# Router logits of thirteen batches as row products on VectorE, and another order of the expert lists with four of the given tiles behind a branch

## The chip, the cores and the metric

The kernel runs on one core of a Trainium2 chip. The metric is the device time of the whole program in microseconds (us), the median of several runs. Instructions run on five engines, each with its own queue: TensorE (PE; its weight loads are shown apart as PEld), VectorE (DVE), ScalarE (ACT), GpSimd (POOL) and SyncE (SP), which here only issues transfers. An engine works its queue in order: what stands behind a waiting instruction waits too.

## The reference

The input x has 16 batches of 256 tokens with 256 features (D); ctx has the same shape. The layers follow each other, each added to x:

```
x = x + xattn0(ctx, layernorm(x))   # 8 heads of 128; keys and values from ctx and x: 512 rows
x = x + ffn0(layernorm(x))          # 1024 hidden units; weights plus a rank-one part made from 16 tokens of the batch
x = x + xattn1(layernorm(x), ctx, ctx)   # one head over 256 rows of ctx
x = x + experts(layernorm(x))       # 8 experts, weights by a router
```

The change touches the last layer. Its router and its experts are:

```
inh = sigmoid(y @ Wr / temperature)       # y = layernorm(x), Wr is 256 x 8: eight logits a token
dist = |inh - 1/e|;  in_zone = lower <= inh <= 0.5
w = exp(-dist/0.1) * in_zone              # zero for experts outside of the zone
w = (two nearest experts with exp(-dist/0.3), where no expert is in the zone);  w = w / sum(w)
out = sum over e of w[e] * (silu(y @ Wg[e]) * (y @ Wu[e])) @ Wd[e]
```

A token needs only the experts with w above zero. The matrices of an expert are 256 x 256. All data are 32-bit floats.

## The kernel before

**Batches and heads.** 16 batches of 8 heads make 128 steps. A step n issues, in this order, the scores of head n (`s1`, PE product `sc`), the division of its softmax rows by their sums on POOL (`s1_scale`), the fetch of the turned rows of head n-1 (`s2_fetch`, `pT`), the queries and keys of head n+1 (`s0q`, `s0k`, `pq` and `pk`), the products with the values of head n-2 (`s3`, `po`), and the turning of head n's rows (`s2`). Turning takes three pieces: DVE transposes blocks of 32 x 32 (`tb`), one transfer of SyncE writes them to DRAM (`hop`), and four transfers read them back in the other order (`pT`). The values `pv` and the preparation of later batches (`inputs`) are spread over the steps by `bulk`. A step takes some 11.3 us, a batch some 91 us.

**What runs between.** The program is written out in a fixed order (no scheduler moves anything). Between the pieces of a step, `gap` (L114) fills in pieces of a list of jobs: each job is a generator that yields the time after which its next piece may be issued, by a rough clock that counts the PE work issued so far (`Clock.pe`, advanced in `mm`, L79, through which every product goes: so nearly all products have line L80; the transposes on PE have L84). For each batch there are two jobs, added when the next batch is at its head 2 (`add_chain`, L1177): `chain(b)` (L345), the rest of that batch's layers, and `route(b)` (L712), its routing.

**The chain of a batch.** In order: the projection `px`; a layer norm; the rank-one part of the feed-forward weights, for which eight rows are written to DRAM and read back as a broadcast to all 128 rows of SBUF (`ev`, two halves of 512 KB; a fetch that is put in `behind_fetch` is issued right behind a head's `pT` fetch) and from which DVE makes `W1e` and POOL and DVE make `W2e`; the products `ph` and `pf`; the second attention (`pq1`, `sc1`, `po1`), for which DVE also makes one product of each row of y with a vector, summed along the row (L551); then the store of x, the layer norm whose rows stand in the tile `row` (256 features, 8 weights, 1 token number), the logits `pl` (L630) and their scaling by 1/temperature into `z` (L637). For the logits of batches 0 to 13 the rows are turned as above (`to_blocks` to `hop_yd_b`, `from_blocks` into `raw`, two copies to `ydT` by `evict`, which takes ACT or DVE by the rough clock); batches 14 and 15 are turned on PE (`turned_tile`, L365). Eight products of 128 x 8 follow with `Wr_sb`. The chain of batch b waits at three places for the chain of batch b-1: before the layer norm of the feed-forward part until `ph` of b-1 is issued (`A.fed`), before od/W1e until `pf` of b-1 is (`A.fed_forward`), and at L522 until the whole chain of b-1 is done. Tiles share buffers by tag: `W1e` has one buffer, and `q1T` is shared by q1T and ydT.

**The routing of a batch.** `route(b)` turns z into the weights (some 30 small operations on ACT and DVE), counts the tokens of each expert with the product `pn`, and gives each token a slot in a list of each expert in DRAM (`slots_d`): 16 indirect transfers on POOL (L804), each of 128 rows of 1060 bytes. A token that an expert doesn't serve is written to the end of that expert's list.

**The experts.** Batches 0 to 11 make part 0, 12 to 15 part 1. The first 1280 rows of each expert's list in part 0 (10 tiles of 128), and the first 512 in part 1 (4 tiles), are always worked; tokens beyond these limits fill spare "given" tiles, six in part 0 and one in part 1 (`UNITS`), whose expert and place are only known at run time (`plan`, L646; class `U`, suffix `_u`). What the given tiles cannot hold goes to loops behind `If beyond` at the end (class `V`). `experts` (L1444) walks a list of groups of one to four tiles (class `G`): a group's rows are loaded (`rows`, three groups ahead), turned through DRAM (`send_rows` two groups ahead: DVE transposes, then `hop_rows_b` on SyncE; `fetch_rows`: `yTd`), and then come the gate `pg` and up `pu` products, `hTd` on DVE, the down products `pd`, one or two groups later, and one indirect transfer per tile on POOL that adds 128 rows to out (L1317). A given tile is turned by PE (`yT_u`, two transposes), has its products `pg_u`, turns h (`hT_u`), and ends with `pd_u` and an indirect transfer; `experts` puts the pieces of a given tile between those of the groups next to it. The order of the lists is:

```
first = groups(0, (4, 3, 3), range(E - 1)) + groups(0, (3, 2, 2, 1, 1, 1), [E - 1])
second = len(first) - 4
lists = first[:-4] + groups(1, (4,), range(E - 1)) + first[-4:-3]
lists += groups(1, (2, 2), [E - 1]) + first[-3:]
units = {second - 1: U(1, 0)}
```

so the last groups of before are a pair of expert 7's part 0, two pairs of its part 1 and three single tiles, and the six given tiles of part 0 stand beside the first six groups of part 1. The last chain and the last routing are also issued into this list, as jobs beside it.

## Time and profile before

| | us |
|---|---|
| median of 3 runs | 1813.56 (1812.45 to 1814.58) |
| profiled execution, own time | 1817.54 |
| its span, first to last instruction | 1815.8 |
| PE busy | 1788.6 (98%) |
| DVE busy | 1201.5 (66%) |
| POOL busy | 838.0 (46%) |
| ACT busy | 589.2 (32%) |
| first and last logits product (`pl`) | 258.8 and 1574.5 |
| routing's transfers (L804), x256 | 291.2 to 1666.5, 962 ns each |
| given tiles' gate and up products (`pg_u`), x28 | 1681.2 to 1768.6, 592 ns each |
| PE clock, mean | 0.998 |

The profile is of one execution, by the hardware's own records. Its page gives for each engine the time in which it ran something ("busy"), the span in 40 slices, the chain of work that ended last, and groups of instructions by line and operation. A line such as "L80 PE MATMUL po<-pT,v 128*128 128x256 f32 x1024 | 242.6, 380 | 3.6" reads: products issued at line 80 that write tile po from tiles pT and v, 1024 of them, busy 242.6 us in sum, 380 ns each in the mean; the engine sat idle 3.6 us in sum just before them, and what follows names the operation that ended that idle time. Products are pipelined: their busy times overlap, so what one costs in a row of them is the distance from its start to the next start. The timeline shows one row for each run of like instructions: start in us, duration, engine and operation, and in square brackets the wait before it.

### The profile page before, as it was taken

Reading aid. Unit: us, or ns where it says so; the run is one execution under the profiler, and the core shown is the slowest. Engines: PE = TensorE matmul, PEld = TensorE weight load, DVE = VectorE, ACT = ScalarE, POOL = GpSimd, SP = SyncE. Lnnn points to the kernel's source line nnn. Section 1 sums busy time; section 2 is a strip of 40 time slices with the busy share of each in tenths; the row PEclk is TensorE's granted clock in tenths of the full one; section 3 lists DMA queues with packets and bytes.
Section 4 is the critical chain, followed back from the end, with each engine's and each line's share of the span. In section 5 each row is a group of like instructions: output and inputs, shape, how many; then the busy total and the mean of one; then the engine's idle time right before and its main releaser. Section 6 shows DMA issues by size and latency. Waiting matters only on the chain.

```text
span 1815.8 us, 22647 instructions
## 1 busy us (share of the span) xinstructions
PE 1788.6 (98%) x6540; PEld 1213.2 (67%) x6540; DVE 1201.5 (66%) x3346; ACT 589.2 (32%) x1316; POOL 838.0 (46%) x983
## 2 busy tenths in 40 slices
PE   8999999999999999999999999999999999999997
PEld 4566676767666666666666666666666677666566
DVE  5465576767676767676767676767666667675554
ACT  3442424243434343434343333333333311211111
POOL 2122225353535344534453435353534357676675
PEclk9999999999999999999999999999999999999999
DMA  6653546565656555656565555556545668899986
GB/s 221 183 180 117 179 133 200 156 197 159 194 162 195 161 190 166 198 158 189 167 191 165 182 173 178 173 181 175 179 153 170 185 179 225 201 252 229 232 158 97
DMA packets 265160, 326.07 MB, mean 180 GB/s; under 512 B 31900, under 2 KB 217672, under 8 KB 265032
## 3 DMA queue, kind: packets, MB, share of 16 engines
q1 hardware_dynamic: 235560, 274.21, 50.3%
q0 software_dynamic: 29424, 50.36, 11.8%
q8 instruction: 54, 0.88, 0.2%
q14 instruction: 74, 0.61, 0.1%
q10 hardware_dynamic: 48, 0.01, 0.0%
HBM read 162.45 MB, written 162.00 MB: 179 GB/s over the span
## 4 chain that ended last, share of the span: by engine, by line
PE 94%; DMA 3%; POOL 1%; DVE 1%; SPq 1%; issue 1%; ACT 0%; POOLq 0%; DVEq 0%; ACTq 0%
PE po L80 14%; PE sc L80 13%; PE pv L80 13%; PE pk L80 12%; PE pq L80 7%; PE px L80 6%; PE ph L80 6%; PE pf L80 6%; PE pg L80 5%; PE pd L80 5%; PE pu L80 5%; DMA hop<-tb 1%; PE pl L80 1%; PE pg_u L80 1%; DMA yTd<-hop_rows_b 1%
## 5 line engine op out<-in xcount | busy, mean ns | idle before, releaser
L980 ACT ACTIVATE pr<-sc,nm 128x512 f32<-128x512 f32 x256 | 173.5, 682 | 483.3 <-DVE nm L974 483.0
L988 POOL TENSOR_SCALAR pr<-pr,ri 128x512 f32<-128x512 f32 x256 | 179.0, 709 | 326.8 <-DVE ri L987 322.3
L804 POOL DMA_INDIRECT slots_d<-row,at_slot x256 | 254.6, 995 | 70.4 <-issue 69.5
L80 PE MATMUL po<-pT,v 128*128 128x256 f32 x1024 | 242.6, 380 | 3.6 <-DVE W2T L1041 1.5
L80 PE MATMUL sc<-kT,qT 128*128 128x512 f32 x512 | 241.0, 593 | 1.5 <-ACT kT L913 1.5
L80 PEld LDWEIGHTS po<-pT,v 128*128 128x128 f32 x1024 | 193.6, 190 | 72.7 <-issue 38.1
L80 PE MATMUL pk<-kvT,Wk_sb 128*128 128x512 f32 x512 | 240.6, 592 | 0.0
L80 PE MATMUL pv<-Wv_sb,kvT 128*128 128x512 f32 x512 | 235.0, 592 | 0.0
L1026 DVE TENSOR_SCALAR outT<-po,cvec 128x256 f32<-128x256 f32 x128 | 61.0, 477 | 242.1 <-PE po L80 242.0
L996 DVE STREAM_TRANSPOSE tb<-pr 128x512 f32<-128x512 f32 x256 | 165.8, 685 | 17.2 <-DMA hop<-tb 17.0
L80 PEld LDWEIGHTS pv<-Wv_sb,kvT 128*128 128x128 f32 x512 | 97.1, 190 | 108.2 <-issue 103.0
L974 DVE TENSOR_REDUCE nm<-sc 128x1 f32<-128x512 f32 x256 | 160.2, 662 | 2.0 <-PE sc L80 1.9
L80 PEld LDWEIGHTS sc<-kT,qT 128*128 128x128 f32 x512 | 97.0, 190 | 69.8 <-issue 61.2
L80 PEld LDWEIGHTS pk<-kvT,Wk_sb 128*128 128x128 f32 x512 | 97.3, 190 | 67.8 <-issue 61.2
L80 PE MATMUL pq<-kvT,Wq_sb 128*128 128x256 f32 x512 | 133.2, 383 | 0.0
L80 PEld LDWEIGHTS pq<-kvT,Wq_sb 128*128 128x128 f32 x512 | 96.6, 191 | 41.8 <-issue 28.2
L80 PE MATMUL px<-Wo_sb,outT 128*128 128x256 f32 x512 | 121.8, 381 | 0.0
L80 PE MATMUL ph<-ybT,W1e 128*128 128x256 f32 x512 | 121.0, 379 | 0.0
L1317 POOL DMA_INDIRECT out_dram<-o,at x65 | 101.8, 1567 | 37.7 <-DVE o L1316 9.3
L450 POOL TENSOR_TENSOR W2e<-ev,od 128x256 f32<-128x256 f32 x120 | 78.5, 681 | 87.7 <-DMA ev<-ev_d 87.7
L80 PE MATMUL pf<-W2e,hT 128*128 128x256 f32 x512 | 118.0, 379 | 0.0
L911 ACT COPY v<-pv 128x512 f32<-128x512 f32 (+1 forms) x132 | 70.6, 536 | 145.4 <-PE pv L80 145.4
(256 smaller groups left out, 2726.6 us busy)
## 6 DMA issues: line engine op xcount, KB each, us to landing
hop<-tb SPq DMA_DIRECT2D x128, 512.0 KB
pT<-hop SPq DMA_DIRECT2D x512, 128.0 KB
ev<-ev_d SPq DMA_DIRECT2D x32, 512.0 KB
rows<-slots_d SPq DMA_DIRECT2D x14, 530.0 KB
hop_rows_b<-rows_b SPq DMA_DIRECT2D x13, 512.0 KB
yTd<-hop_rows_b SPq DMA_DIRECT2D x52, 128.0 KB
rows<-slots_d SPq DMA_DIRECT2D x15, 397.5 KB
hop_rows_b<-rows_b SPq DMA_DIRECT2D x14, 384.0 KB
```

The costliest lines, as they stand in the source:

```text
L80: nc.tensor.matmul(out, lhsT, rhs, **kw)
L450: (nc.gpsimd if b < B - 1 else nc.vector).tensor_tensor(W2e[:, c, d, :].rearrange("p (i a) -> p i a", i=NI), evs[1][:, :, c * NA : (c + 1) ...
L804: ins = nc.gpsimd.indirect_dma_start(out=slots_d[part], out_offset=bass.IndirectOffsetOnAxis(ap=at_slot[:, c, e : e + 1], axis=0), in_=row ...
L911: nc.scalar.copy(out, src)
L974: nc.vector.tensor_reduce(nm, sc, AX.X, ALU.max, negate=True)
L980: nc.scalar.activation(pr, sc, AF.Exp, bias=nm, accum_out=sm)
L988: nc.gpsimd.tensor_scalar(pr, pr, ri, 1.0, ALU.mult, ALU.mult)
L996: nc.vector.transpose(tb[:, :, c, :], heads[n][c][0].rearrange("p (m f) -> p m f", m=QP))
L1026: nc.vector.tensor_scalar(o, po, col("bv", h), None, ALU.add)
L1317: ins = nc.gpsimd.indirect_dma_start(out=out_rows[0 : sum(NTOKS[: self.part + 1]), :], out_offset=bass.IndirectOffsetOnAxis(ap=self.at[:, ...
```

## The change

Four things change.

**Logits.** Batches 0 to 12 (`b < B - 3`) no longer turn the rows of the last layer norm and make no `pl`. The router matrix is copied once, at batch 0's head 5, into a DRAM tile `WrT_d` with a row for each expert (L1167). For each of these batches SyncE broadcasts it to all 128 rows of SBUF in two halves of 512 KB (`Wr_all`, in the buffer of `W1e`, fetched behind a head's pT), and DVE makes 16 row products with sums (L653: for each expert and half batch, 256 elements a row), whose sums are the logits. They are then scaled by 1/temperature. The elementwise products go to an unused tile in the buffer of `q1T`. Batch 13 now takes the way of 14 and 15: turned on PE, then `pl`.

**Waits.** The chain of b-1 need not be done at L531 (L522 before), only its second attention (`A.attended`); two new waits hold the making of `W1e` until the logits of b-2 are issued, and of `q1T` until those of b-1 are (`A.scored`). `Wr_all` is made only once `ph` of the next batch is issued (`A.fed`), since they share a buffer.

**Given tiles.** Two of part 0's six given tiles and the one of part 1 stay in the list (`AMONG`). The other four are worked at the end behind a branch, which is taken if the tokens beyond the limits need more than two tiles in part 0 or one in part 1; the loops of class `V` stand in a second branch inside it. `plan` makes a second flag, and both are loaded into registers.

**Lists.** Expert 7's part 0 is cut into 3, 2, 1, 1, 1, 1, 1. The five single tiles stand one by one behind the groups of four of part 1, from expert 2 to expert 6; the two pairs of part 1 of expert 7 end the list. The two given tiles of part 0 stand beside the first two groups of part 1.

```diff
--- before.py
+++ after.py
@@ -163,6 +163,8 @@
     NTOKS = [n * S for n in PARTS]
     CAPS = [10 * P, 4 * P]
     UNITS = (6, 1)
+    AMONG = (2, 1)
     NU = sum(UNITS)
     NM = max(n - k for n, k in zip(NTOKS, CAPS)) // P
@@ -248,6 +250,10 @@
     g0 = keep.tile([P, 1], F32, name="g0")
     WvT = keep.tile([P, DC, D], F32, name="WvT")
     Wr_sb = keep.tile([P, DC, E], F32, name="Wr_sb")
+    WrT_d = dram.tile([E, D], F32, tag="WrT_d", bufs=1, name="WrT_d")
+    zero = keep.tile([P, 1], F32, name="zero")
+    nc.gpsimd.memset(zero, 0.0)
@@ -427,6 +433,9 @@
             yield 0.2
         yield max(landed[0], there) - Clock.pe
         while behind is not None and b - 1 not in A.fed_forward:
+            yield 0.4
+        while b >= 2 and b - 2 not in A.scored:
             yield 0.4
@@ -519,7 +528,7 @@
         rs = ln_rstd(mv, "q")
         yield queued - 0.3
-        while behind is not None and not behind.done:
+        while behind is not None and b - 1 not in A.attended:
             yield 0.4
         y = wk.tile([P, TC, D], F32, tag="y", name=f"yc_{b}")
         ln_apply(y, x_b, mv, rs)
@@ -553,6 +562,8 @@
                 scale=1.0, scalar=g0, accum_out=rc[:, c : c + 1],
             )
         yield there - Clock.pe
+        while behind is not None and b - 1 not in A.scored:
+            yield 0.4
         q1T = wk.tile([P, DC, S], F32, tag="q1T", name=f"q1T_{b}")
         for m in range(DC):
             pq = mm_tile(S, f"pq1_{b}_{m}")
@@ -601,6 +612,7 @@
                 x_b[:, c, :], po, ri, x_b[:, c, :], ALU.mult, ALU.add
             )
             stats(c, "d", mv)
+        A.attended.add(b)
         rs = ln_rstd(mv, "d")
@@ -611,33 +623,58 @@
         row = A.row[b] = wk.tile([P, TC, ROW], F32, tag="row", bufs=2, name=f"row_{b}")
         ln_apply(row[:, :, 0:D], x_b, mv, rs)
         nc.vector.tensor_copy(row[:, :, D + E], number[:, b * TC : (b + 1) * TC])
-        if hopped:
-            hop = to_blocks(wk, row, TC, "tbc", 2, f"yd_{b}_b")
-            yield SENT
-            raw = raw_tile("raw_c", f"ydT_{b}")
-            from_blocks(raw, hop)
-            yield LANDED
-            ydT = wk.tile([P, DC, S], F32, tag="q1T", name=f"ydT_{b}")
-            for d in range(DC):
-                evict(ydT[:, d, :], in_order(raw)[:, d], None, None)
-            yield 4.0
+        if b < B - 3:
+            while b + 1 not in A.fed:
+                yield 0.4
+            Wr_all = wk.tile([P, E, D], F32, tag="W1e", name=f"Wr_all_{b}")
+            landed = []
+            def wr_everywhere(half):
+                nc.sync.dma_start(
+                    Wr_all[:, ts(half, E // 2), :].rearrange("p e d -> p (e d)"),
+                    WrT_d[ts(half, E // 2)].rearrange("e d -> (e d)").partition_broadcast(P),
+                )
+                landed.append(Clock.pe + 8.0)
+            behind_fetch.extend([lambda: wr_everywhere(0), lambda: wr_everywhere(1)])
+            while b >= 1 and b - 1 not in A.weighed:
+                yield 0.4
+            z = A.z[b] = wk.tile([P, TC, E], F32, tag="z", name=f"z_{b}")
+            part_of = wk.tile([P, D], F32, tag="q1T", name=f"zy_{b}", padded_shape=[P, DC * S])
+            for e in range(E):
+                if e % (E // 2) == 0:
+                    half = e // (E // 2)
+                    while len(landed) <= half:
+                        yield 0.2
+                    yield landed[half] - Clock.pe
+                for c in range(TC):
+                    nc.vector.tensor_tensor_reduce(
+                        out=part_of, in0=row[:, c, 0:D], in1=Wr_all[:, e, :], op0=ALU.mult,
+                        op1=ALU.add, scale=1.0, scalar=zero, accum_out=z[:, c, e : e + 1],
+                    )
+                yield 2.2
+            z = z.rearrange("p t e -> p (t e)")
+            nc.vector.tensor_scalar(z, z, lasting["invt"], None, ALU.mult)
         else:
             yield 1.4
             ydT = turned_tile(row, "q1T", f"ydT_{b}")
             yield 1.6
-        while b >= 1 and b - 1 not in A.weighed:
-            yield 0.4
-        pl = mm_tile(TC * E, f"pl_{b}")
-        for c in range(TC):
-            for d in range(DC):
-                mm(
-                    pl[:, ts(c, E)], ydT[:, d, ts(c, P)], Wr_sb[:, d, :],
-                    start=(d == 0), stop=(d == DC - 1),
-                )
-        A.z[b] = wk.tile([P, TC, E], F32, tag="z", name=f"z_{b}")
-        nc.vector.tensor_scalar(
-            A.z[b].rearrange("p t e -> p (t e)"), pl, lasting["invt"], None, ALU.mult
-        )
+            while b >= 1 and b - 1 not in A.weighed:
+                yield 0.4
+            pl = mm_tile(TC * E, f"pl_{b}")
+            for c in range(TC):
+                for d in range(DC):
+                    mm(
+                        pl[:, ts(c, E)], ydT[:, d, ts(c, P)], Wr_sb[:, d, :],
+                        start=(d == 0), stop=(d == DC - 1),
+                    )
+            A.z[b] = wk.tile([P, TC, E], F32, tag="z", name=f"z_{b}")
+            nc.vector.tensor_scalar(
+                A.z[b].rearrange("p t e -> p (t e)"), pl, lasting["invt"], None, ALU.mult
+            )
+        A.scored.add(b)
     class Plan:
@@ -673,7 +710,12 @@
         for k, n in enumerate(UNITS):
             nc.vector.tensor_scalar(over[:, k : k + 1], till[:, k, E - 1 : E], float(n), None, ALU.is_gt)
         nc.vector.tensor_tensor(over[:, 0:1], over[:, 0:1], over[:, 1:2], ALU.max)
-        nc.vector.tensor_copy(beyond, over[:, 0:1])
+        nc.vector.tensor_copy(beyond[:, 1:2], over[:, 0:1])
+        more = tmp("more_units", [P, 2])
+        for k, n in enumerate(AMONG):
+            nc.vector.tensor_scalar(more[:, k : k + 1], till[:, k, E - 1 : E], float(n), None, ALU.is_gt)
+        nc.vector.tensor_tensor(more[:, 0:1], more[:, 0:1], more[:, 1:2], ALU.max)
+        nc.vector.tensor_copy(beyond[:, 0:1], more[:, 0:1])
         half = tmp("half", [P, 1])
         nc.vector.tensor_scalar(half, over[:, 0:1], -0.5, 0.5, ALU.mult, ALU.add)
@@ -706,7 +748,7 @@
             ALU.mult,
         )
-    beyond = const.tile([P, 1], I32, name="beyond")
+    beyond = const.tile([P, 2], I32, name="beyond")
     def route(b, A, mine):
@@ -816,7 +858,8 @@
     class A:
         xs, ctxT, outT, cin, kvT, v = {}, {}, {}, {}, {}, {}
         row, z = {}, {}
-        projected, fed, fed_forward, weighed = set(), set(), set(), set()
+        projected, fed, fed_forward, attended = set(), set(), set(), set()
+        scored, weighed = set(), set()
         tails = {}
@@ -1121,6 +1164,7 @@
             if h == 5:
                 nc.sync.dma_start(Wo_sb, Wo.rearrange("(h p) d -> p h d", p=P))
                 nc.sync.dma_start(Wr_sb, Wr.rearrange("(c p) e -> p c e", p=P))
+                nc.sync.dma_start(WrT_d, Wr.rearrange("d e -> e d"))
                 lasting["b2"] = row_everywhere(b2, "b2_bc")
                 lasting["bv1"] = row_everywhere(Wv_b, "bv1_bc")
                 lasting["scale"] = row_everywhere(ffn_scale, "scale_bc")
@@ -1524,13 +1568,17 @@
-        first = groups(0, (4, 3, 3), range(E - 1)) + groups(0, (3, 2, 2, 1, 1, 1), [E - 1])
-        second = len(first) - 4
-        lists = first[:-4] + groups(1, (4,), range(E - 1)) + first[-4:-3]
-        lists += groups(1, (2, 2), [E - 1]) + first[-3:]
+        first = groups(0, (4, 3, 3), range(E - 1)) + groups(0, (3, 2) + (1,) * 5, [E - 1])
+        second = len(first) - 5
+        lists, singles = first[:second], first[second:]
         units = {second - 1: U(1, 0)}
-        for j in range(UNITS[0]):
+        for j in range(AMONG[0]):
             units[second + 1 + j] = U(0, j)
+        for e in range(E - 1):
+            lists += groups(1, (4,), [e])
+            if e >= AMONG[0]:
+                lists.append(singles.pop(0))
+        lists += groups(1, (2, 2), [E - 1])
         last = None
         for n in range(NS + 2):
@@ -1591,18 +1639,29 @@
         some = nc.values_load(beyond[0:1, 0:1], min_val=0, max_val=1)
+        all_slots = nc.values_load(beyond[0:1, 1:2], min_val=0, max_val=1)
         with tc.If(some > 0):
             for part in range(2):
-                with tc.For_i(0, E) as e:
-                    with tc.For_i(0, (NTOKS[part] - CAPS[part]) // P, 2) as t:
-                        pair = [V(part, e, t + j, j) for j in range(2)]
-                        for v in pair:
-                            v.load()
-                        for v in pair:
-                            v.turn()
-                            v.gates()
-                            v.turn_h()
-                            v.down()
+                for j in range(AMONG[part], UNITS[part]):
+                    u = U(part, j)
+                    u.load()
+                    u.turn()
+                    u.gates()
+                    u.turn_h()
+                    u.down()
+            with tc.If(all_slots > 0):
+                for part in range(2):
+                    with tc.For_i(0, E) as e:
+                        with tc.For_i(0, (NTOKS[part] - CAPS[part]) // P, 2) as t:
+                            pair = [V(part, e, t + j, j) for j in range(2)]
+                            for v in pair:
+                                v.load()
+                            for v in pair:
+                                v.turn()
+                                v.gates()
+                                v.turn_h()
+                                v.down()
 # ---- launch: one core; inputs and outputs as the reference has them ----
```

## The prediction

> **What bounds the kernel now.** I read the page first. TensorE (PE) is busy in all 40 slices at full clock, and the chain that ended last lies on it for 94%. So a microsecond of PE work taken out is worth a microsecond, as long as nothing new makes PE wait; and work on VectorE (DVE, 66%) costs nothing until PE waits for it.
>
> ```profile
> span 1815.8 us, 22647 instructions
> PE 1788.6 (98%) x6540; PEld 1213.2 (67%) x6540; DVE 1201.5 (66%) x3346; ACT 589.2 (32%) x1316; POOL 838.0 (46%) x983
> PE 94%; DMA 3%; POOL 1%; DVE 1%; SPq 1%; issue 1%; ACT 0%; POOLq 0%; DVEq 0%; ACTq 0%
> L80 PE MATMUL po<-pT,v 128*128 128x256 f32 x1024 | 242.6, 380 | 3.6 <-DVE W2T L1041 1.5 <-DMA pT<-hop 1.2 <-issue 0.9
> L551 DVE CUSTOM_DVE_ANT_0 pr<-yc,g,g 128x256 f32<-128x256 f32 x32 | 14.9, 502 | 0.0
> ```
>
> Then the timeline of PE, for the price of each removed piece. PE's busy times overlap, so I price by starts: next start minus own start. The columns are start, duration, engine and operation. The logits (pl) take 532.63 to 533.44, 0.81. In the last stage a spare given tile (suffix _u) takes 0.86 for pd_u, 1.72 for pg_u and 0.22 each for yT_u and hT_u: 3.02.
>
> ```profile
> 532.63 0.95 PE L80 MATMUL pl<-Wr_sb,ydT 128*128 128x8 f32 x8
> 533.44 1.11 PE L80 MATMUL pq<-kvT,Wq_sb 128*128 128x256 f32 x4
> ...
> 1738.01 1.03 PE L80 MATMUL pd_u<-wx_all,hT_u 128*128 x4
> 1738.88 1.89 PE L80 MATMUL pd<-wx_all,hTd 128*128 128x256 f32 x8
> 1740.60 1.88 PE L80 MATMUL pg_u<-wx_all,yT_u 128*128 x4
> 1742.32 1.88 PE L80 MATMUL pg<-yTd,wx_all 128*128 128x512 f32 x4
> ...
> 1745.75 0.38 PE L84 MATMUL yT_u<-ident,rows_u 128*128 128x128 f32 x2
> 1745.97 1.89 PE L80 MATMUL pd<-wx_all,hTd 128*128 128x256 f32 x8
> 1747.70 0.38 PE L84 MATMUL hT_u<-ident,h_u 128*128 128x128 f32 x2
> 1747.92 1.88 PE L80 MATMUL pg<-yTd,wx_all 128*128 128x512 f32 x4
> ...
> 1796.73 0.68 PE L80 MATMUL pg<-yTd,wx_all 128*128 128x128 f32 x4 [0.55 <-DMA yTd<-hop_rows_b]
> 1802.19 0.87 PE L80 MATMUL pg<-yTd,wx_all 128*128 128x128 f32 x4 [2.57 <-DMA yTd<-hop_rows_b]
> ```
>
> The last two lines are the end: three single tiles in a row have too little work between them to hide the turning of the next one's rows through DRAM. Last, a table by stretches of one batch. The columns are stretch, its length, busy times of PE, PEld, DVE, ACT and POOL with counts, clock, DMA share, GB/s. Here a delay would hurt: at 486 to 497 the DMA engines are 93% busy, and just behind it PE loses 0.5.
>
> ```profile
> 475.00:486.00 11.00, 11.00 (x37) 6.68 (x36) 8.31 (x23) 5.69 (x15) 7.70 (x9) 1.00 0.49 175
> 486.00:497.00 11.00, 11.00 (x34) 6.17 (x33) 4.96 (x12) 4.48 (x12) 6.97 (x8) 1.00 0.93 261
> 497.00:508.00 11.00, 10.54 (x40) 7.25 (x39) 6.34 (x17) 4.04 (x11) 5.29 (x6) 1.00 0.78 235
> 542.00:554.00 12.00, 12.00 (x46) 8.31 (x45) 10.99 (x37) 2.93 (x8) 4.86 (x6) 1.00 0.42 131
> ```
>
> **The change part by part.** All against the profiled execution, 1817.54 with a span of 1815.8; it lies 3.98 above the median of 1813.56, and I take the same difference off both.
>
> 1. Logits of batches 0 to 12 off PE: 13 x 0.81 = -10.5, all on the path.
>
> 2. What replaces them. Each batch gets 16 row products (L653) of the kind of L551, 502 ns, or 0.41 from start to start where they follow each other: 6.6 to 8.0. DVE loses two row transposes (0.76) and two copies of ydT (1.30, 26 of 28 were on DVE). So DVE gains 4.5 to 6 per batch of 91, 70 over the run: 71% of the span. They are queued in pairs between other work, over some 35 us, and the routing that follows comes some 20 us of PE work later. In the changed order the crowded stretches (542 to 554) give up that routing in exchange for the products, so they get no fuller. The load moves to the stretch between the transposes of heads 2 and 3 (476.9 to 484.4 here, 7.4 long). It held 5.8 of DVE work; the routing adds two blocks, 1.6 and 2.4 long where they run now, so 9.8: 2.4 too much, and up to 0.8 more is late from five routing steps ahead of head 2. Head 3's transposes end some 3 us late, and SyncE's queue behind them (hop of head 3, ybT, pT of head 3) with them. What covers this: the routing's 16 scatters (L804, 128 rows x 1060 bytes = 136 KB each) now run from 473 to 500 and put nine of them, 1.2 MB, beside the 2 MB that heads 2 and 3 need between 482.8 and 493.6; in the new order they come some 20 us later. 2 MB at 261 GB/s take 7.7 where 10.8 are spent now: 3 us, as much as DVE loses. Bounds: a gain of 2.1 (the 3.6 that PE waits before po, less the 1.5 of W2T at the start); a loss of 13 x 3.2 = 42 if the scatters relieved nothing. I take -1.0, since both effects are read from the same stretch and are equal, and heads 4 to 0 of the next batch have slack (their pT are fetched 11 us and more before po).
>
> 3. SyncE per batch: two broadcasts of 512 KB (Wr_all, L635) for the 256 KB to and from DRAM of hop_yd_b and ydT, five issues. They wait for the W1e buffer that the next batch's ph has read, and are issued beside pT in stretches with a DMA share near 0.45; ev of the same size and path made DVE wait 0.8 in total. Zero, cover: the 10 us between issue and first product. The new waits (next q1T and W1e behind the products) start no sooner than now: pq1 and ph stand at the same PE work within 4 us. Zero.
>
> 4. Batch 13 turns its row on PE: +0.44 to +0.71 (batches 14, 15) and a wait of 0 to 1.5; its own wait today before pl, 1.4, goes. Zero.
>
> 5. WrT_d (L1167), once in batch 0: 2048 single elements. Wr_sb beside it, 256 pieces, held SyncE's queue for 1.19, a plain 1 MB load 0.40; so 0.4 to 9.5 of queue, ahead of hop of head 5. That head has 1.6 of idle queue before it, and 13.0 from its fetch (75.35) to po (88.33), where head 7 needs at most 5.7 (94.68 to 100.37, no wait): 8.9 of cover. Price 0 to 5, taken 0.5, near the cover. The Trainium skill, "DMA: Bandwidth & Descriptors", section "Rules for kernel authors", speaks against this line: a last dimension that isn't contiguous becomes one descriptor per element, and rearranging by access pattern is put at 19 times the proper transpose. By that rule the upper end, 9.5 of queue, holds, and the sum would be 0.6 worse than with a plain load, as the trace's cover leaves only that.
>
> 6. Four given tiles leave the main list: 4 x 3.02 = -12.1. Their work on other engines was hidden. The reference's routing on these inputs fills 1340 and 1297 rows for two experts of the first part (limit 1280, next 1276) and 516 for one of the second (limit 512, next 452): two tiles and one, what stays in the list, so the branch isn't taken. A pair of expert 7 becomes two singles: 2 x 1.78 - 3.45 = +0.1.
>
> 7. The end. From 1795.9 to the last matmul PE loses 5.7: 3.3 waiting, the rest at a clock of 0.86. The singles now stand between groups of four, and two pairs end the list. New waits: the last pair's hTd, 0.7; and each group of four behind a single has 9.5 of PE work for turning its rows, which takes 2.25 to the hop's issue, 2.6 to 3.0 to its landing and 4.3 to 6.3 for the fetch: 0 to 2 each, three times, taken 0.7. So 5.7 - 2.8 = -2.9; bounds -5 and +1.
>
> 8. After the last matmul: two rows of outputs follow each other on POOL (1.54 each) instead of one, +0.7; a second register load (0.50 on POOL), +0.5. Together +1.2.
>
> Sum: -10.5 - 1.0 + 0.5 - 12.1 + 0.1 - 2.9 + 1.2 = **-24.7**: 1792.8 for a profiled execution, 1788.9 for the median.
>
> **The rivals.**
> A, slower: the wait for head 3. If the scatters relieve nothing, po of heads 2 and 3 waits up to 3.2 in each of 13 batches: 1788.9 + 1.0 + 42 = 1832. It decides from 2.0 a batch. For it: PE already waits at that place in some batches. Against it: the DMA share of 0.93 there, which falls.
> B, half the gain: the same wait at 0.5 to 1.0 a batch (6 to 13), or a slow WrT_d (5) with full waits in the list (4): 1796 to 1803.
> C, the branch is taken: four tiles one after another with nothing between. The rows of one make a chain of 0.22 + 0.37 + 1.72 + 0.38 + 0.84 + 0.22 + 0.37 + 0.86 + 0.44 + 1.54 = 7.0, and 3 for its load: 40, so 1829. Against it: the counts above.
> D, no change: PE was not the limit in the last stage, so that six of the removed tiles' microseconds or all twelve return as waits for POOL, which holds 107 of 156 us there. Even then the logits' 10.5 stay: 1801.
>
> **How the numbers follow.** The forecast as summed, with its own range 1782 to 1796: 0.70. B and D together: 0.18. A: 0.09, of which a third ends below no change. C: 0.02. Better than 1782: 0.01. So 1782 to 1803 holds about 0.87 of it, which I keep for the unknown size of step 2. A measurement of this kernel tells 0.2% (3.6 us) from no change; faster: 0.70 + 0.18 + 0.01 and a little of A = 0.90, same 0.02, slower 0.08.
>
> **What would show it.** Step 1: pl x24 instead of x128. Step 2: 208 rows of L653, DVE near 1270; idle before po no more than 3.6; in the stretch of heads 2 and 3 DMA share below 0.9, and the scatters behind it. Step 6: pg_u x12. Step 7: waits of pg for yTd in the list below 4 in sum, none of 2.6 at the end. It is wrong if po shows idle of tens of microseconds behind pT, or if the tiles of u2 to u5 appear after the branch.

## The result: slower by 1.3%

| | before | after |
|---|---|---|
| median of four runs | 1814.07 | 1836.84 (1835.07 to 1838.44) |
| ratio, 95% interval | | 1.0127 [1.0115, 1.0140] |
| profiled execution, span | 1817.54, 1815.8 | 1838.44, 1836.7 |

The forecast was 24.7 less; it became some 23 more. The page after, to be read against the lines shown of before:

```profile
span 1836.7 us, 22540 instructions
PE 1778.0 (97%) x6408; PEld 1195.6 (65%) x6408; DVE 1278.4 (70%) x3695; ACT 584.0 (32%) x1304; POOL 846.1 (46%) x980
PE 59%; DVE 16%; POOL 12%; issue 5%; DMA 5%; ACT 3%; SPq 1%; ACTq 0%; DVEq 0%; POOLq 0%
L80 PE MATMUL po<-pT,v 128*128 128x256 f32 x1024 | 244.7, 382 | 10.1 <-ACT kT L956 7.2
L80 PE MATMUL sc<-kT,qT 128*128 128x512 f32 x512 | 242.6, 596 | 8.1 <-ACT kT L956 8.1
L80 PE MATMUL pf<-W2e,hT 128*128 128x256 f32 x512 | 124.8, 385 | 4.3 <-DVE W2e L467 4.3
```

The same two products in the page of before, which the prediction does not show:

```profile
L80 PE MATMUL sc<-kT,qT 128*128 128x512 f32 x512 | 241.0, 593 | 1.5 <-ACT kT L913 1.5
L80 PE MATMUL pf<-W2e,hT 128*128 128x256 f32 x512 | 118.0, 379 | 0.0
```

On the page PE's busy time fell by 10.6 only, since products at a slow clock count as longer work (the mean clock was 0.992, where it was 0.998). The third line says more: the chain that ended last lay on PE for 94%, and now does for 59%, with DVE and POOL in it for 28%.

So I split PE's timeline. For each product I take the time from its start to the next start, and subtract the median of that form in the same trace. What is over (if more than 0.06) is stall: waiting, and the slow clock that follows it. The rest is work.

| part of the span | before | after | change | predicted |
|---|---|---|---|---|
| PE's work | 1778.8 | 1756.4 | -22.4 | -22.5 (steps 1 and 6) |
| stall in batch 0 | 4.9 | 14.7 | +9.8 | +0.5 (step 5) |
| stall in batches 1 to 13 | 5.6 | 20.8 | +15.2 | -1.0 (step 2) |
| stall where the experts' list starts (1373 to 1461 before, 1387 to 1493 after) | 1.75 | 17.05 | +15.3 | none |
| stall in the last stage | 10.8 | 9.9 | -0.9 | -2.9 (step 7) |
| behind the last matmul | 7.8 | 11.3 | +3.6 | +1.2 (step 8) |

With 0.4 at the start these make the 20.9 between the spans. The removed work was sized to a tenth of a microsecond. Everything that went wrong is waiting. A row of stall also differs between executions of the same code: in two later kernels that are alike up to the experts' list (g1 and h1), batches 1 to 13 lost 5.8 and 2.9. So changes of 3 and less in one row say little.

**Batch 0.** From the timeline after (start, duration, engine or queue, line, operation), head 5's hop, its pT, the next transposes on DVE, and the product po with the last work of ACT before it:

```profile
76.13 0.36 SPq L1043 DMA_DIRECT2D hop<-tb  x1
91.59 1.74 SPq L1052 DMA_DIRECT2D pT<-hop  x4
91.63 1.30 DVE L1039 STREAM_TRANSPOSE tb<-pr 128x512 f32<-128x512 f32 x2 [9.99 <-DMA hop<-tb]
95.30 0.69 ACT L956 ACTIVATE kT<-pk,cvec 128x512 f32<-128x512 f32 x1
96.08 1.19 PE L80 MATMUL po<-pT,v 128*128 128x256 f32 x2 [7.24 <-ACT kT L956]
```

And the same in before, where po had no wait:

```profile
71.75 0.33 SPq L1000 DMA_DIRECT2D hop<-tb  x1
75.35 1.75 SPq L1009 DMA_DIRECT2D pT<-hop  x4
88.33 1.89 PE L80 MATMUL po<-pT,v 128*128 128x256 f32 x8
```

Between a hop and its fetch lay 3.6 before (71.75 to 75.35); here it is 15.5. pT's fetch is 16.2 later than before: 4.4 of this is the hop's own later issue, since the four loads that SyncE issued behind the copy took 7.65 in sum, where they took 2.92 before. PE waits 7.24 ahead of po; some 2 more go in a low clock behind it. The profile puts the wait down to ACT's kT (95.30 to 95.99), but two waits end there within 0.1: pT's last piece landed at 95.95. Both come from the late hop. pT is read from it, and DVE's next transposes waited 9.99 for it to land; the row maxima behind them on DVE, and ACT's kT behind those, came late with them. In between the core's DMA moved little, as the first row of this table by stretches shows (length; busy times of PE, PEld, DVE, ACT, POOL; clock; DMA share; GB/s). At 76 to 80 it moved 196 GB/s before, and here 7; from 80 to 92 it moved 55 to 67, where it had moved 67 to 178:

```profile
76.00:80.00 4.00, 4.00 (x12) 2.03 (x11) 0.41 (x1) 1.17 (x2) 0.00 (x0) 1.00 0.85 7
486.40:497.40 11.00, 11.00 (x37) 6.68 (x36) 10.34 (x39) 5.70 (x15) 2.74 (x3) 1.00 0.22 85
497.40:508.40 11.00, 11.00 (x36) 6.18 (x35) 6.21 (x16) 4.07 (x10) 1.36 (x2) 1.00 0.78 229
```

**Batches 1 to 13.** The other two rows are the transposes of heads 2 and 3, the place that step 2 feared for. DVE is at 10.34 of 11, the DMA share fell from 0.93 to 0.78, and po loses nothing there; over batches 1 to 13 its stall went from 3.6 to 2.8. The loss stands 40 us further on, before sc (9.8) and pf (7.3), which lost nothing in these batches before. One batch's stretch in the timeline after, POOL, DVE and PE together:

```profile
531.08 1.19 POOL L459 TENSOR_TENSOR W2e<-ev,od 128x256 f32<-128x256 f32 x2
...
541.75 0.96 POOL L846 DMA_INDIRECT slots_d<-row,at_slot  x1 [0.30 <-issue]
542.74 1.19 POOL L459 TENSOR_TENSOR W2e<-ev,od 128x256 f32<-128x256 f32 x2
543.29 1.03 PE L80 MATMUL pf<-W2e,hT 128*128 128x256 f32 x4
543.96 0.69 DVE L467 TENSOR_TENSOR W2e<-W2e,W2T 128x512 f32<-128x512 f32 x1 [3.12 <-POOL W2e L459]
544.71 1.13 PE L80 MATMUL pf<-W2e,hT 128*128 128x256 f32 x4 [0.39 <-DVE W2e L467]
...
561.93 1.98 PE L80 MATMUL sc<-kT,qT 128*128 128x512 f32 x4 [0.58 <-ACT kT L956]
```

In before the last of these adds on DVE (W2e) waits for nothing and is done 3.0 ahead of the pf products that stand in this place:

```profile
530.72 0.67 DVE L458 TENSOR_TENSOR W2e<-W2e,W2T 128x512 f32<-128x512 f32 x1
534.39 1.89 PE L80 MATMUL pf<-W2e,hT 128*128 128x256 f32 x8
```

The 16 scatters of rows to slots (L846, 1.27 from start to start) ran in a free part of POOL's queue before; moved later, 12 of them stand ahead of the W2e products that POOL makes for the next pf, and 4 among them. DVE then waits 3.12 for the last product, pf's second half waits for DVE, and the steps queued on DVE come late, and with them kT and sc 17 us on. A typical batch lost 0.17 and now loses 1.59.

**Start of the experts' list.** The same, once, at the largest size: POOL's list of W2e products comes behind batch 12's scatters, DVE is idle for 4.87 and late for the copies of the first experts' rows (yTd). The first line is of before, where the add waits for nothing, the others of after:

```profile
1439.98 0.68 DVE L458 TENSOR_TENSOR W2e<-W2e,W2T 128x512 f32<-128x512 f32 x1
...
1455.04 5.05 POOL L459 TENSOR_TENSOR W2e<-ev,od 128x256 f32<-128x256 f32 x8
1456.27 3.36 DVE L467 TENSOR_TENSOR W2e<-W2e,W2T 128x512 f32<-128x512 f32 x1 [4.87 <-POOL W2e L459]
1465.08 1.65 PE L80 MATMUL pg<-yTd,wx 128*128 128x384 f32 x2 [7.00 <-DVE yTd L958]
```

**Last stage.** Two groups of four behind single tiles wait for their rows; behind the second PE also loses 1.7 at a low clock (before, the waits for single tiles at the end were 0.55 and 2.57):

```profile
1770.23 1.95 PE L80 MATMUL pg<-yTd,wx_all 128*128 128x512 f32 x4 [2.85 <-DMA yTd<-hop_rows_b]
1785.45 2.81 PE L80 MATMUL pg<-yTd,wx_all 128*128 128x512 f32 x4 [2.01 <-DMA yTd<-hop_rows_b]
```

Of the 3.6 that the end grew, 1.2 lie ahead of POOL's last output, which starts 2.0 behind the last matmul where it started 0.8 behind it. The other 2.3 lie behind that output's start (9.3 to the end of the span, 7.0 before), and no run separates them.

### The profile page after: what moved, and what is told of

It reads as the page before. It is cut to its first block, busy times and chain, and to the rows that moved or that the text cites. A ratio compares the mean times of both kernels' runs of the same rounds, so it can differ in the third digit from the quotient of the medians.

```text
span 1836.7 us, 22540 instructions
## 1 busy us (share of the span) xinstructions
PE 1778.0 (97%) x6408; PEld 1195.6 (65%) x6408; DVE 1278.4 (70%) x3695; ACT 584.0 (32%) x1304; POOL 846.1 (46%) x980
## 4 chain that ended last, share of the span: by engine, by line
PE 59%; DVE 16%; POOL 12%; issue 5%; DMA 5%; ACT 3%; SPq 1%; ACTq 0%; DVEq 0%; POOLq 0%
PE sc L80 8%; PE po L80 8%; PE pv L80 7%; POOL slots_d L846 7%; PE pk L80 6%; PE px L80 6%; PE pq L80 5%; PE pg L80 4%; PE pu L80 4%; PE pd L80 4%; DVE tb L1039 3%; POOL W2e L459 2%; PE ph L80 2%; PE pf L80 2%; DMA hop<-tb 2%
## 5 line engine op out<-in xcount | busy, mean ns | idle before, releaser
L1031 POOL TENSOR_SCALAR pr<-pr,ri 128x512 f32<-128x512 f32 x256 | 195.8, 775 | 428.6 <-DVE ri L1030 425.8
L846 POOL DMA_INDIRECT slots_d<-row,at_slot x256 | 257.9, 1008 | 72.1 <-issue 70.3
L80 PE MATMUL po<-pT,v 128*128 128x256 f32 x1024 | 244.7, 382 | 10.1 <-ACT kT L956 7.2
L80 PE MATMUL pf<-W2e,hT 128*128 128x256 f32 x512 | 124.8, 385 | 4.3 <-DVE W2e L467 4.3
L653 DVE CUSTOM_DVE_ANT_0 zy<-row,Wr_all,zero 128x256 f32<-128x256 f32 x208 | 124.4, 598 | 4.6
L80 PEld LDWEIGHTS pf<-W2e,hT 128*128 128x128 f32 x512 | 97.5, 192 | 34.7 <-issue 14.0
```

The costliest lines, as they stand in the source:

```text
L80: nc.tensor.matmul(out, lhsT, rhs, **kw)
L653: nc.vector.tensor_tensor_reduce(out=part_of, in0=row[:, c, 0:D], in1=Wr_all[:, e, :], op0=ALU.mult, op1=ALU.add, scale=1.0, scalar=zero, ...
L846: ins = nc.gpsimd.indirect_dma_start(out=slots_d[part], out_offset=bass.IndirectOffsetOnAxis(ap=at_slot[:, c, e : e + 1], axis=0), in_=row ...
L1031: nc.gpsimd.tensor_scalar(pr, pr, ri, 1.0, ALU.mult, ALU.mult)
```

## The experiments

Kernels of one group ran on the same chip. The kernel before took 1812.9 to 1819 on the five chips, so ratios to it are compared across groups; 0.001 is 1.8 us. In the edits, ... stands for lines left out.

### First group: each suspected place by itself

Theory: four separate losses, the strided copy (10), the scatters in POOL's queue together with the missing cover (the per-batch stall), the list's start, and the list's waits. Rivals: POOL's queue alone explains the batches; the new list brings nothing.

**e1_turned_router**: after, with WrT_d made by PE, and stored as 8 rows of 1 KB.

```diff
-                nc.sync.dma_start(WrT_d, Wr.rearrange("d e -> e d"))
+                for d in range(DC):
+                    turned(wr_ps[0:E, ts(d, P)], Wr_sb[:, d, :], ident)
+                nc.vector.tensor_copy(WrT_sb, wr_ps[0:E, :])
+                nc.sync.dma_start(WrT_d, WrT_sb)
```

> The changed kernel with another making of WrT_d: Wr_sb is turned on PE (two transposes of 128 x 8) at batch 0's head 7 and stored as 8 rows of 1 KB; the strided copy of 2048 single elements is gone. Theory: the copy's elements stood on the DMA engines ahead of a head's hop, po waited 7.4 and PE then ran 2.0 slower than its pace: the stall of batch 0 falls from 14.7 to about 5 as before the change, so 1836.8 - 9.8 = 1827 (1825 to 1830). Rival: the wait comes from the other loads of that head (Wo_sb, the broadcasts), which are there in the kernel before too, or comes back one head later: 1834 to 1838.

Measured 1826.83, ratio 1.0070 [1.0053, 1.0087]: 10 less than after. Batch 0's stall fell from 14.7 to 5.5. In its timeline hop and fetch are 2.7 apart, and po follows without a wait:

```profile
82.98 0.34 SPq L1043 DMA_DIRECT2D hop<-tb  x1
85.66 1.74 SPq L1052 DMA_DIRECT2D pT<-hop  x4
89.01 1.89 PE L80 MATMUL po<-pT,v 128*128 128x256 f32 x8
```

So the copy of 8 KB in single elements cost 10 us; its rival, the other loads of that head, is out, since e1 has them too.

**e2_late_slots**: after, with the scatters of b held until pf of b+2 has been issued (in `route`).

```diff
+        while b + 2 < B and b + 2 not in A.fed_forward:
+            yield 0.4
```

> The changed kernel, with the 16 slot transfers of batch b held until pf of batch b+2 is issued, so behind the W2e products on POOL; all 208 row products stay. Theory POOL's queue: the slot transfers (1.27 from start to start) stand ahead of W2e, DVE waits 3.1 for W2e with tb and nm queued behind it, and ACT's kT comes late: the 0.55 before pf and 0.74 before sc go in 12 batches (15), and so does most of the 14 of stalls at 1457 to 1475: 1836.8 - 15 - 12 = 1810 (1805 to 1817). Rival, DVE is full: the products are as many, the waits stay: 1833 to 1840. Third: the transfers collide with something else in their new place (row of the next batch, hops of the second attention): 1815 to 1835, with new waits of po or pq1 behind DMA.

Measured 1859.32, 1.0251 [1.0234, 1.0268], far above what was expected. The batches did what the theory says: the stall of one fell from 1.59 to 0.54, DVE's wait for W2e and pf's are gone, and the list's start lost 3.6 instead of 17. But the last batches' scatters came so late that part 1's first rows weren't there, and the last stage lost 54.6:

```profile
1727.22 0.66 PE L84 MATMUL yT_u<-ident,rows_u 128*128 128x128 f32 x2 [23.82 <-DMA rows_u<-slots_d]
```

**e5_before_slots_at_w2e**: before, with its scatters held until they stand among the W2e products.

```diff
+                if i == 0:
+                    A.feeding.add(b)
...
+        while b + 2 < B and b + 2 not in A.feeding:
+            yield 0.4
```

> The kernel before, with one thing changed: the 16 slot transfers of batch b are held until the second pair of ph of batch b+2, which puts them ahead of and among the W2e products on POOL, as the changed kernel has them; no row products, no Wr_all, logits on PE. Theory POOL's queue: the same waits come, 1.2 in each of some 12 batches and some of the 14 at the start of the experts' list: 1814 + 15 + 0 to 14 = 1829 to 1843. Rival, the row products on DVE are needed for it: 1813 to 1818. Gain at the same time: the DMA share at heads 2 and 3 falls, and po's waits there (2 in sum) go.

Measured 1837.62, 1.0131 [1.0114, 1.0148]. The total lies in the expected range, but for another reason: a batch's stall stays at 0.17, and what is lost is lost in the last stretches (7.8 and 26.3, yT_u waiting as in e2). Yet DVE waits for POOL as it does after:

```profile
532.49 0.95 PE L80 MATMUL pl<-Wr_sb,ydT 128*128 128x8 f32 x8
533.30 1.11 PE L80 MATMUL pq<-kvT,Wq_sb 128*128 128x256 f32 x4
533.35 0.69 DVE L458 TENSOR_TENSOR W2e<-W2e,W2T 128x512 f32<-128x512 f32 x1 [2.89 <-POOL W2e L450]
534.24 1.89 PE L80 MATMUL pf<-W2e,hT 128*128 128x256 f32 x8
```

The difference is what PE has to do meanwhile. Here pl and pq, 1.75 together, stand between sc and this pf. The last W2e is ready at 534.04, 0.2 ahead of pf's start and some 1.1 ahead of its second half, which reads it. After, pl is gone, and pf is issued in its place, ahead of pq: pf's first half follows sc at once. By this sum its second half comes 1.75 earlier and so some 0.7 too early; a stall of 0.66 is measured. pl's own 0.81 alone would just not have uncovered the wait; pq's new place behind pf did the rest. So POOL's queue alone isn't enough: the removed logits, with pq behind them, were the cover of a wait that their own removal's reordering makes. (Two limits of this test: 6 of its 16 scatters run behind the last W2e, and it has no row products. In g3 the wait before pf stays with row products of a quarter of the size.)

**e4_old_lists**: after, with the list of before and the four tiles behind the branch.

```diff
-        first = groups(0, (4, 3, 3), range(E - 1)) + groups(0, (3, 2) + (1,) * 5, [E - 1])
+        first = groups(0, (4, 3, 3), range(E - 1)) + groups(0, (3, 2, 2, 1, 1, 1), [E - 1])
+        lists = first[:-4] + groups(1, (4,), range(E - 1)) + first[-4:-3]
+        lists += groups(1, (2, 2), [E - 1]) + first[-3:]
```

> The changed kernel with the list of before: expert 7's part 0 as 3, 2, 2, 1, 1, 1, a pair of it ahead of expert 7's pairs of part 1, the three singles at the end; the four given tiles stay behind the branch. Theory: single tiles between groups of four cost two waits of 3.0 and 2.2 and a stretch at low clock of 1.7, with 0.7 more at the end; the old end costs 5.7, less the pair made of two singles (0.1) and one row of outputs less on POOL at the end (1.5 to 2.4): 1836.8 - 3.5 = 1833 (1831 to 1835). Rival: without the four given tiles as filling, the old end is no better and POOL's outputs pile up: 1836 to 1842. Second rival: the list isn't worth anything either way: 1836 to 1838.

Measured 1837.24, 1.0133 [1.0116, 1.0150]: the same as after. PE ends 7.8 earlier (1817.57 against 1825.39), but 16.8 follow, where after has 11.3: POOL's outputs pile up, 1.85 from one start to the next.

```profile
1816.87 0.70 PE L80 MATMUL pd<-wx_all,hTd 128*128 128x256 f32 x2 [0.20 <-issue]
1823.11 1.54 POOL L1361 DMA_INDIRECT out_dram<-o,at  x1 [0.30 <-issue]
1824.95 1.54 POOL L1361 DMA_INDIRECT out_dram<-o_more,at  x1 [0.30 <-issue]
```

So the rival holds here: the new order of the list, against the old one with the four tiles out, moves the loss between PE and POOL, and is worth nothing in sum.

### Second group: repairs in sequence, and the list alone

**f1_products_to_11**: e1, with row products up to batch 11 (`if b < B - 4:` for `b < B - 3`), so that batch 12 scatters early.

> The changed kernel with the turned router matrix of e1_turned_router (1826.8 by itself), and batch 12 turned on PE as batches 13 to 15 are, so that 12 batches have row products. Theory: the 15.5 of stalls where the experts' list begins come from batch 12's 16 slot transfers standing ahead of W2e of batch 14 on POOL; with batch 12's logits earlier they are done before: 1826.8 - 14 + 1.3 (pl and four transposes on PE) - 1.4 (one batch less of the waits before pf and sc) = 1812.7 (1810 to 1816). Rival: the stall comes from DVE's or ACT's own load there, since the experts' first rows and the last chain meet: 1825 to 1829.

1822.49, 1.0036 [1.0023, 1.0049], less than half of the gain that was expected: the list's start lost 8.7 instead of 15.5. What is left was laid to DVE, where the routing of batch 13 stands ahead of the yTd copies; i1 tests that.

**f2_hold**: f1, with e2's wait for batches 0 to 10 only.

```diff
+        while b + 2 < B - 3 and b + 2 not in A.fed_forward:
+            yield 0.4
```

> As f1_products_to_11, and the slot transfers of batches 0 to 10 held until pf of the batch two later is issued, so behind its W2e on POOL; those of the last batches are not held. Theory: of the 1.4 in each of some 11 batches the 0.55 before pf and half of the 0.74 before sc go, as in e2_late_slots (1.59 to 0.54 a batch): f1 - 11.5 = 1801 (1799 to 1804), and the lost time at the end of e2_late_slots (54 in the last stretch, where the last tokens' slots came late) isn't there. Rival: the held transfers push the routing of the last batches back even so, by the chain of routings: over 1806.

1814.90, 0.9987 [0.9975, 0.9999], 7.6 less than f1, where 11.5 was expected. A batch still loses 0.54 to 1.4. In the traces batches 1 to 13 lost 11.7 less than in f1, as expected; the list's start and the last stage lost some 4 more.

**f3_lists_alone**: before, with the list and the branch of after; the logits stay on PE.

```diff
+    AMONG = (2, 1)
...
-        first = groups(0, (4, 3, 3), range(E - 1)) + groups(0, (3, 2, 2, 1, 1, 1), [E - 1])
+        first = groups(0, (4, 3, 3), range(E - 1)) + groups(0, (3, 2) + (1,) * 5, [E - 1])
```

> The kernel before with the second half of the change alone: four given tiles behind the branch, expert 7's five single tiles between the groups of four; logits as before, on PE. Theory, from the two traces' last stretch: PE work -12.0, stalls -0.9, after the last matmul +3.6: 1814.4 - 9.3 = 1805 (1803 to 1808). By the prediction's steps 6 to 8 it would be 1814.4 - 13.7 = 1800.7. Rival, the last stretch is bound by POOL's outputs whatever PE does: 1811 to 1815.

1813.32, 0.9982 [0.9972, 0.9991]. Steps 6 to 8 had promised 13.7; they give 3.3 (1.6 to 5.1 by the interval). That is less than the 6 to 11 expected of this run too, and what its rival has. In the trace PE's work fell by 12.2, as promised. Two groups of four behind single tiles wait as in after (1.88 and 2.02), and the last stage lost 12.6, 1.8 more than before; 11.35 follow the last matmul, 3.6 more:

```profile
1741.26 3.20 PE L80 MATMUL pg<-yTd,wx_all 128*128 128x512 f32 x4 [1.88 <-DMA yTd<-hop_rows_b]
```

With this the change divides into three: list and branch -3.3 (f3), strided copy +10.3 (after less e1), all else of the logits +16 (e1 less f3). They make the +23 by construction, since each is the difference of two neighbours; what each is worth is known to some 2 to 3 us.

**f4_pairs_between**: f2, with pairs between the groups of four in place of singles.

```diff
-        first = groups(0, (4, 3, 3), range(E - 1)) + groups(0, (3, 2) + (1,) * 5, [E - 1])
+        first = groups(0, (4, 3, 3), range(E - 1)) + groups(0, (3, 3, 2, 2), [E - 1])
...
-            if e >= AMONG[0]:
+            if e in (3, 5):
```

> As f2_hold, with expert 7's part 0 cut into 3, 3, 2, 2 and the two pairs put between groups of four of part 1 (after experts 3 and 5) in place of the five singles. Theory: a group of four behind a single waits for its rows since the single gives only 2.6 of PE work to hide the transfer; a pair gives 5.2, so the waits of 3.0 and 2.2 and the 1.7 at low clock behind them go: f2 - 6 = 1795 (1793 to 1798). Rival: with five groups of four in a row POOL's outputs (1.85 each and some 3.5 between experts) become the bound and stay behind at the end, as with the old list in e4_old_lists, where PE ended 7.8 earlier and the end came 5.4 later behind it: f2 - 1 to f2 + 3.

1808.71, 0.9960 [0.9948, 0.9972]: 6.2 less than f2, as expected. The list's stalls fell to 2.2, but 14.4 now follow the last matmul.

### Third group: are the row products worth anything, and why do batches wait?

Two theories on f4. One: the products on DVE still lose more than they save, so before's logits with f4's list must be better than f4. The other: they save about what they lose by now.

**g1_before_with_pairs**: f3, with f4's list. **g4_before_pairs_later**: g1, with the second pair one expert later (`if e in (3, 6):`).

> The kernel before with its logits on PE, four given tiles behind the branch and the list with pairs of f4_pairs_between; no row products. Theory: the row products, even with the router matrix turned and the slot transfers held, lose more (some 14 in stalls of PE) than the 9 of PE work they save, so without them f4 - 4: PE work -12.1, stalls in the list -8.5 as in f4, after the last matmul +6.7: before - 14 = ratio 0.9923 (0.990 to 0.995), under f4's 0.996. Rival: the two parts need each other, and the list without the row products is as f4 or slower: 0.996 to 0.999.

> As g1_before_with_pairs, with the second pair of expert 7's part 0 behind the group of expert 6 instead of expert 5. Theory: at the end POOL stays behind PE (f4: 14.4 from the last matmul to the end) and waits 2.9 for expert 6's outputs to land before expert 7's; three pairs of outputs that don't depend on each other in between hide that wait: g1 - 2 to g1 - 3. Rival: PE then waits for the rows of the first of three pairs in a row, or POOL's wait comes back elsewhere: g1 - 1 to g1 + 2.

1812.29, 0.9972 [0.9960, 0.9985], and 1811.38, 0.9961 [0.9948, 0.9973]: neither better than f4, so the first theory fell, and the row products earn about what they lose; the difference between the two is within their intervals. What they share is an end of 17.3 and 17.7 behind the last matmul. In g1, POOL is the one that is late (DVE's last o is ready at 1793.7):

```profile
1774.36 1.54 POOL L1324 DMA_INDIRECT out_dram<-o,at  x1 [4.65 <-DMA out_dram<-o_more,at]
...
1793.21 0.48 DVE L1323 TENSOR_SCALAR o_more<-pd,wt 128x256 f32<-128x256 f32 x1 [0.38 <-PE pd L80]
1795.57 1.54 POOL L1324 DMA_INDIRECT out_dram<-o,at  x1 [3.00 <-DVEq L1606]
1801.11 1.54 POOL L1324 DMA_INDIRECT out_dram<-o_more,at  x1 [0.30 <-issue]
```

**g3_quarter_products**: f1, with products over 64 of the 256 features, so that DVE is relieved and POOL's queue is not (its logits differ, so the branches at the end are taken and the one run took 3739.1; only the stretches ahead of the list are read).

```diff
-                        out=part_of, in0=row[:, c, 0:D], in1=Wr_all[:, e, :], op0=ALU.mult,
+                        out=part_of[:, 0:64], in0=row[:, c, 0:64], in1=Wr_all[:, e, 0:64], op0=ALU.mult,
```

> f1_products_to_11 with row products over 64 of the 256 features (and twice the scale), so the logits aren't the reference's, other tokens go to the experts, and the branch at the end may be taken: only the stretches up to the experts' list are read. It takes some 0.25 from each of 192 products, and nothing from POOL. Theory, two causes: the 0.55 before pf stays (W2e late behind the slot transfers on POOL), the 0.74 before sc goes to 0 to 0.2 (DVE catches up before nm): 1.59 a batch falls to 0.8. Rival, POOL's queue alone: both stay, 1.5 to 1.6. Rival, DVE's load alone: both go, 0.2.

A product took 285 ns instead of 485, and a batch lost 0.80, as two separate causes demand. The later wait, of sc, is gone with the DVE work; the wait for W2e is as long as ever:

```profile
623.28 0.69 DVE L467 TENSOR_TENSOR W2e<-W2e,W2T 128x512 f32<-128x512 f32 x1 [3.12 <-POOL W2e L459]
624.03 1.13 PE L80 MATMUL pf<-W2e,hT 128*128 128x256 f32 x4 [0.39 <-DVE W2e L467]
640.51 1.94 PE L80 MATMUL sc<-kT,qT 128*128 128x512 f32 x4
```

So of a batch's 1.59, the 0.66 before pf is POOL's queue in front of W2e: it goes in e2 and stays here. The 0.85 before sc is DVE, too full to catch up: of it 0.06 is left here. The late W2e adds to it, since e2, with DVE as full as after, leaves 0.46.

### Fourth group: POOL's outputs at the end

**h1_fewer_outputs**: g1, without 8 of its 115 outputs (tiles 2 and 3 of part 1, experts 3 to 6). **h2_three_pairs**: f4, with 4, 2, 2, 2 and pairs behind experts 2, 4 and 6.

```diff
+                if self.part == 1 and 3 <= self.e <= 6 and t >= 2:
+                    return
```
```diff
+        first = groups(0, (4, 3, 3), range(E - 1)) + groups(0, (4, 2, 2, 2), [E - 1])
...
+            if e in (2, 4, 6):
```

> g1_before_with_pairs without 8 of its 115 outputs: the indirect transfers of tiles 2 and 3 of part 1's experts 3 to 6 are left out (their products and scalings stay), so these rows of out are not complete. Theory: in that kernel POOL's outputs end the program: POOL is 7 to 10 behind DVE in the whole last stage, and 17.3 pass from the last matmul to the end, 7.8 in the kernel before. 8 x 1.85 = 14.8 less on POOL ends its lag: 17.3 falls to about 8, PE's end stays at 1793, so before x 0.9972 - 9 = ratio 0.992. Rival: the end is set by PE's last tiles and by the last outputs' landing, and POOL's lag costs nothing: 0.996 to 0.998.

> f4_pairs_between with expert 7's part 0 as 4, 2, 2, 2 and its three pairs behind experts 2, 4 and 6 of part 1. Theory: POOL waits 3.0 to 4.8 each time that the next output belongs to another expert of the same part, until the last one's rows have landed; a pair of the other part between two experts covers that. One more place covered, and the one ahead of expert 7: POOL ends 3 to 6 earlier, and PE isn't changed: f4 (ratio 0.996) - 3 to 5 = 0.9935 to 0.9945. Rival: POOL's lag at the end is the same, as between g1 and g4: 0.995 to 0.997.

h1: 1799.79, 0.9936 [0.9921, 0.9951]. The 17.3 behind the last matmul became 10.3, and POOL now waits for DVE's o, not the other way round:

```profile
1781.65 1.54 POOL L1326 DMA_INDIRECT out_dram<-o,at  x1 [3.52 <-DVE o L1323]
```

So in the last stage POOL's outputs are a second limit that lies just behind PE. (PE's last matmul also came 7.6 earlier in h1's trace, 6.2 of it by less stall in stages ahead of the last one, which the edit leaves as they were. So the size rests on the ratios: 0.0036 between g1 and h1, each with an interval of some 0.0014 to either side.)

h2: 1813.99, 1.0005 [0.9996, 1.0014], where a gain was expected. With one more pair moved back, part 1 starts earlier, and yT_u waits 8.2 for rows of the slots, which the last scatters (to 1667.9) fill. The two limits close on each other, and the list has little room between them.

### Fifth group: a better kernel

**i1_rows_by_act**: f4, with the yTd copies of the first two groups of the list by ACT (`nc.scalar.copy` in place of `evict`), which take them off DVE where the list starts.

> f4_pairs_between with one thing changed: the first two groups' rows (yTd) are copied out of PSUM by ACT in place of DVE (two copies move). Theory: what is left of the stall at the start of the experts' list, some 9 in f4 (3.1 and 2.7 before pg, and a low clock behind them), is DVE's queue: the two yTd copies stand behind 9 of routing work of batch 13, which the change put there, and behind W2e; ACT has nothing from 1437.8 to 1447.3. The copies then come right after the gelu: stall of that stretch 11.5 to about 4, and 1808.7 - 5 (f4's ratio 0.996 to 0.993), less what POOL's lag at the end (6.6 in f4) gives back: 0.993 to 0.995. Rival: the wait only moves to the next product behind DVE's queue (hTd, W2e for pf), stall 9 to 12, ratio 0.9955 to 0.997.

1800.61 (1798.93 to 1802.12), 0.9900 [0.9883, 0.9918]: faster than both kernels, by more than expected. The list's start lost 3.6 (11.5 in f4), and PE is busy for 98%, as in before:

```profile
PE 1768.9 (98%) x6374; PEld 1191.2 (66%) x6374; DVE 1282.6 (71%) x3644; ACT 585.2 (33%) x1301; POOL 846.3 (47%) x980
```

No run gives the same copies to a kernel with its logits on PE; in g1, which has them there, the list's start loses only 3.4.

## Why the prediction was wrong, by its steps

**Steps 1 and 6 held**: 22.5 of PE work promised, 22.4 found; pl x24, pg_u x12, and the branch isn't taken. They say how much work PE is spared, which isn't what the run saves.

**Step 2 failed, and decided.** Its reasoning on heads 2 and 3 was right as far as it went: DVE is fuller, the DMA share fell, and po's stall in batches 1 to 13 fell by 0.8, where -1.0 was taken (of its 10.1 of idle time on the page 7.2 are batch 0's). But it counted only what moving the 16 scatters takes away from that stretch, and not where they go: into POOL's queue ahead of the W2e products, 16 x 1.27 = 20 us. It costed the place of DVE and of the DMA engines and never asked for POOL's. And it took pl as 0.81 of pure cost, while pl, with pq issued behind it, was also the cover of pf's wait for W2e (e5). It also held that the crowded stretches get no fuller; at 553.4 to 565.4 DVE is busy for 11.79 of 12, and there sc waits (before, 542 to 554 had 10.99). Together +15.2 in the batches where -1.0 was summed, and, by the last of the same moves, part of the +15.3 at the list's start, which had no step at all. e2 takes two thirds of the per-batch part away, g3 halves it, and e5 shows that POOL's queue does nothing where pl and pq stand ahead of pf. At the list's start f1 and i1 show batch 12's scatters and DVE's yTd copies as causes; how much each holds in after isn't separated further. (Two readings of step 2 were slightly off and change nothing: the row of scatters ran to 503.5, not 500, and DVE was busy for 5.35 of the stretch, not 5.8.)

**Step 5 was mis-sized.** The copy itself held SyncE's queue for 0.82, near the low bound, and the four loads behind it for 4.7 more. But most of the price fell on the transfers behind: the hop landed 15.4 after its issue, and pT's fetch came 16.2 late, against a cover of 8.9 and an upper bound of 9.5. Nor did the step look at the other wait on that hop, of DVE's next transposes. Taken 0.5, measured 9.8. The Trainium skill, "DMA: Bandwidth & Descriptors", section "Rules for kernel authors", says that a last dimension that isn't contiguous becomes one descriptor per element. The trace agrees: between 60 and 100 the core's packets of under 512 bytes rose from 1075 to 2912, and e1, without the copy, has 1076. I had weighed the trace's cover more.

**Steps 7 and 8.** Waits of pg were foreseen at 0 to 2 each and came at 2.85 and 2.01, the second with 1.7 of slow clock behind it: -0.9 for -2.9. The end cost 3.6 for 1.2. By f3 steps 6 to 8 are worth 3.3 of the 13.7. Of the 10.4 that are missing, its trace shows 4.7 as stall in the last stage (1.8 more, where 2.9 less was summed) and 2.4 at the end; the rest stays open. That POOL was the limit in the last stage is the mechanism of rival D: its outputs follow each other at 1.85 and wait 3 to 4.8 at a change of expert until the last expert's rows have landed, and e4 and h1 show that they hold the end. D had found the right engine and stopped at 1801, since it left the logits' 10.5 untouched.

**Rival A** had the sign and nearly the size (1832), by the wrong wait: it looked for pT in heads 2 and 3. That its size is near is luck. The test that I named, tens of microseconds of idle time before po, would have cleared the change: po has 10.1, most of it in batch 0, and the rest of the idle time lies before sc, pf and pg.

## What to carry to other kernels

A transfer that is moved can cost more at its new place than it frees at the old one: note what stands behind it on the queue of the engine that issues it, at the new place, and who waits for that. Before taking work off the engine that bounds the kernel, ask which late operands it was covering: price the removed work against the slack of what follows it, and not only by its length. An engine at 46% over the span, as POOL here, may be the limit in the one stage where the gain is to be had; so count its issues per tile against the bounding engine's time per tile, in that stage.

## What the runs showed of the hardware that wasn't expected

- A copy of 8 KB, DRAM to DRAM, in 2048 single elements held SyncE's queue for only 0.82. But for 8 us (72 to 80) the core's DMA moved 7 GB/s, with a DMA share of 0.85 in the second half, where before it moved 140 and 196; a hop issued behind it landed after 15.4.
- An add of two SBUF tiles on DVE took 3.36 in the line at 1456.27, beside eight products of POOL; the median of the 64 such adds is 0.69. The Trainium skill, "SBUF — State Buffer", section "Who interferes with whom", says that DVE and GpSimd share a pair of ports under an exclusive lock. The row agrees with it, but no run separated it.
- An indirect transfer of an output that adds to DRAM took 1.54 on POOL, 1.85 from start to start, with up to 4.65 of waiting until the one before had landed: 8 fewer of them were worth 0.0036 of the time, about 6.5 (h1 against g1, give or take some 3.6), and the stretch behind the last matmul became 7.0 shorter.
